# Flamingo gated cross-attention: two of the additions of the softmax sums are made by adding transfers issued from GpSimd

## The chip, the cores and the metric

The kernel runs on one core of a Trainium2 chip. The metric is the device time of one execution in microseconds. The kernel before takes 2557.49 us (median of 2 runs, 2556.8 and 2558.18).

## The reference

Four batches of 256 query rows attend to 1601 context rows each, with 32 query heads of width 128 that share 8 key and value heads, in float32. A gated feed-forward block with eight low-rank experts follows.

```python
x = x + tanh(g_xattn[0]) * xattn(layernorm(x), ctx_4096, Wq, bq, Wkv, bkv, Wo, bo)
x = x + tanh(g_ffn[0]) * ffn(layernorm(x), base_W, router_W, lora_A, lora_B)

# xattn
q = (query @ Wq + bq).reshape(B, L, NKV, G, HDIM)
k_, v_ = split(kv @ Wkv + bkv, 2, axis=-1)          # reshaped to (B, Lk, NKV, HDIM)
scores = einsum('blkgd,bmkd->bkglm', q, k) * scale
attn = softmax(scores, axis=-1)
o = einsum('bkglm,bmkd->blkgd', attn, v).reshape(B, L, NHEAD * HDIM)
return o @ Wo + bo
```

The change touches the denominators of the softmax: for every query row and head, the sum of the exponentials over 1601 keys.

## The kernel before, in words

**Groups.** One group is a key `(b, h, l)`: a batch, a key head and a half of the 256 query rows. There are 4 x 8 x 2 = 64 groups. A group has 4 heads x 128 rows = 512 columns (`W`), and the 1601 keys lie on the partitions in 13 tiles: one of 65 rows and twelve of 128. The twelve go in pairs, so a group has 7 pieces, j = 0 (the 65 rows alone) and j = 1 to 6 (two key tiles each, a tile `p` of 128 x 2 x 512 float32, 512 KB).

**Score phase.** `run_group(cur, prev)` alternates pieces of the current group's scores (`score_unit`, L1142: TensorE writes `sc` to PSUM, ScalarE copies it to `p` in L1151, VectorE folds `p` into a running maximum `mx`, L1067, L1070, L1073) with pieces of the previous group's product with the values (`av_unit`, L1233).

**Softmax.** `softmax(key)` then lets VectorE reduce `mx` across partitions and spread the result (`spread`, L1106 to L1100, five steps), subtract it from every `p` (L1181), and ScalarE take the exponentials (L1184). The sums of the exponentials are pieces in a queue `sum`: `sum_piece(key, j)` calls `fold`, where j = 2 adds `p[1]`, `p[2]` (L1067) and `p[0]` (L1070) into a tile `sm` of 128 x 2 x 512, and j = 3, 4, 5, 6 each add one more `p` (L1073). After the last, `sum_spread` puts the five spreading steps of `sm` in the queues: L1106 adds the halves, L1107 transposes blocks, L1086 reduces and GpSimd copies quadrants (L1090); L1093 and L1209 reduce and invert, GpSimd copies again (L1097); L1100 spreads the result to `rb`. `normalize` (L1292) multiplies the product with it. There is one buffer of `sm`, one of `mx`, and 9 of `p`. The last two keys, `(3, 7, 0)` and `(3, 7, 1)`, have no spreading of `sm`: TensorE sums it across partitions with a matrix of ones (L1257, `su_steps`), and the last key's j = 6 is never folded.

**Projections.** Between score phases `window` runs steps of tasks on TensorE: the query, key and value projections (L896, L907) and the output projection (L484, L1310). A projection pair works with seven products and three PSUM banks; ScalarE copies some products out (L941, L944) and VectorE adds others to them (L951), and TensorE writes on into a bank after such an evacuation has read it.

**Order.** The order of instructions on TensorE, VectorE and ScalarE is fixed while the program is built. A planner keeps a clock for each of them. `later` queues a piece with an engine, a duration in ns, and a key that it waits for; `take` runs the piece, moves the engine's clock by the duration, and marks the piece's own key as done at the end plus `SEM` (200 ns). `fit`, `pump` and `force` take pieces from the heads of the queues, the earliest possible start first, and of equal starts the earlier queue in the list `sub, oT, so, exp, ln, T, norm, sum, low, low_a`. The engines then execute in that order, each instruction behind its semaphores, whatever the real times are. GpSimd's queue holds the small copies of the spreading (six a group), a few memsets (L533, L663) and a few loads (L231 to L234, L558, L601); the large loads and stores are issued from SyncE.

Of the kernel before, what the change touches and what calls it, by code (L numbers as in the profile page):

```python
# [12 lines left out]
ALU = mybir.AluOpType  # L13
# [14 lines left out]
def flamingo_kernel(  # L28
# [51 lines left out]
    nc = tc.nc  # L80
# [16 lines left out]
    NPAIR = len(pairs)  # L97
# [20 lines left out]
    SEM = 200  # L118
    GP_COPIES = 800
    FIT = 300  # L120
    NEVER = math.inf
    clock = {"now": 0.0, "v": 0.0, "a": 0.0, "hold": 0.0}
    free = [0.0] * NBANK
    done = {}
    queues = {q: deque() for q in ("sub", "oT", "so", "exp", "ln", "T", "norm", "sum", "low", "low_a")}

    def vec(ns, ready=None):

        clock["v"] = max(clock["v"], clock["now"] + SEM if ready is None else ready) + ns
        return clock["v"] + SEM  # L130
# [5 lines left out]
    def later(queue, engine, ns, ready, fn, key=None):  # L136

        queues[queue].append((engine, ns, ready, fn, key))

    def start_of(piece):  # L140
        engine, _, ready, _, _ = piece
        if not isinstance(ready, float):
            ready = done.get(ready, NEVER)
        return max(clock[engine], ready)

    def take(q):

        piece = q.popleft()
        engine, ns, _, fn, key = piece
        start = start_of(piece)  # L150
        fn()
        clock[engine] = start + ns
        if key is not None:
            done[key] = start + ns + SEM + (GP_COPIES if key[0] == "part" and key[2] < 4 else 0)

    def pump(until=NEVER, most=None):

        n = 0
        while most is None or n < most:
            heads = [(start_of(q[0]), i, q) for i, q in enumerate(queues.values()) if q]  # L160
            if not heads:
                return n
            start, _, q = min(heads)
            if start == NEVER or start + min(q[0][1], 1200) / 2 > until:
                return n
            take(q)
            n += 1
        return n
# [78 lines left out]
    def mm_cost(n):  # L247

        return 2 * (max(n, P) / 1.2 + 2)
# [809 lines left out]
    p_t, oT_t, rb_t, av_t, po_t = {}, {}, {}, {}, {}  # L1059

    def fold(acc, op, j, key):


        p = p_t[key]
        first = NPAIR - FULL // 2
        if j == first + 1:
            nc.vector.tensor_tensor(acc, p[first], p[first + 1], op)  # L1067
            if first:
                r = rows[-1]
                nc.vector.tensor_tensor(acc[:r, 0, :], acc[:r, 0, :], p[0][:r, 0, :], op)  # L1070
                return 1930
        elif j > first + 1:
            nc.vector.tensor_tensor(acc, acc, p[j], op)  # L1073
        else:
            return 0
        return 1220

    def spread(acc, op, nm, res, after=None, eng=nc.vector):

        q = small.tile([P, 4, NB], F32, tag="quad", name=f"quad_{nm}", bufs=2)
        m = small.tile([P, NB], F32, tag="quadm", name=f"quadm_{nm}", bufs=2)

        def quadrants():
            nc.vector.tensor_reduce(  # L1086
                q[:, 0, :], acc[:, 1, :].rearrange("p (c k) -> p c k", k=32), AX.X, op
            )
            for a in range(1, 4):
                eng.tensor_copy(q[:32, a, :], q[32 * a : 32 * a + 32, 0, :])  # L1090

        def whole():
            nc.vector.tensor_reduce(m[:32], q[:32].rearrange("p a c -> p c a"), AX.X, op)  # L1093
            if after is not None:
                after(m[:32])
            for a in range(1, 4):
                eng.tensor_copy(m[32 * a : 32 * a + 32], m[:32])  # L1097

        def back():
            nc.vector.transpose(  # L1100
                res.rearrange("p (c k) -> p c k", k=32), m.unsqueeze(2).to_broadcast([P, NB, 32])
            )

        own = 550 if eng is nc.vector else 0
        return [
            (690, lambda: nc.vector.tensor_tensor(acc[:, 0, :], acc[:, 0, :], acc[:, 1, :], op)),  # L1106
            (710, lambda: nc.vector.transpose(acc[:, 1, :], acc[:, 0, :])),  # L1107
            (690 + own, quadrants),
            (250 + own + (270 if after is not None else 0), whole),
            (710, back),  # L1110
        ]
# [47 lines left out]
    acc_t, sum_t, late, ring = {}, {}, [], []  # L1159
# [4 lines left out]
    def softmax(key):  # L1164

        nm = "_".join(map(str, key))
        while queues["sub"]:
            pump(most=1)
        mb = pool.tile([P, W], F32, tag="mb", name=f"mb_{nm}", bufs=1)
        for ns, fn in spread(acc_t[key], ALU.max, f"mx_{nm}", mb):  # L1170
            fn()
            vec(ns, clock["v"])

        clock["hold"] = clock["v"] + 1500 - 3 * mm_cost(W)
        for j, tiles in enumerate(pairs):
            n, r = len(tiles), rows[tiles[-1]]
            p = p_t[key][j][:r, :n, :]

            def sub(p=p, r=r, n=n):
                m = mb[:r].unsqueeze(1).to_broadcast([r, n, W])  # L1180
                nc.vector.tensor_tensor(p, p, m, ALU.subtract)  # L1181

            def exp(p=p):
                nc.scalar.activation(p, p, AF.Exp, scale=scale)  # L1184

            later("sub", "v", 1140 if n > 1 else 690, clock["v"], sub, ("sub", key, j))
            later("exp", "a", 1060 if n > 1 else 630, ("sub", key, j), exp, ("exp", key, j))
            if key == last and j == NPAIR - 1:
                continue
            first = NPAIR - FULL // 2  # L1190
            ns = 0 if j <= first else 1230 if j > first + 1 else 1970 if first else 1230
            later("sum", "v", ns, ("exp", key, j), lambda j=j: sum_piece(key, j), ("sum", key, j))
        if key not in tail_keys:
            later("sum", "v", 0, 0.0, lambda: sum_spread(key), ("sums", key))

    def sum_piece(key, j):
        if j == 0:
            nm = "_".join(map(str, key))
            tag = "mx" if key == last else "sm"
            acc_t[key] = pool.tile([P, 2, W], F32, tag=tag, name=f"sm_{nm}", bufs=1)  # L1200
        fold(acc_t[key], ALU.add, j, key)

    def sum_spread(key):

        nm = "_".join(map(str, key))

        rb_t[key] = pool.tile([P, W], F32, tag="rb", name=f"rb_{nm}", bufs=1)
        parts = spread(
            acc_t[key], ALU.add, f"sm_{nm}", rb_t[key], lambda m: nc.vector.reciprocal(m, m), nc.gpsimd  # L1209
        )  # L1210
        for i, (ns, fn) in reversed(list(enumerate(parts[:3]))):
            queues["sum"].appendleft(("v", ns, 0.0, fn, ("part", key, i)))
        for i in (3, 4):
            later("norm", "v", parts[i][0], ("part", key, i - 1), parts[i][1], ("part", key, i))
        later("norm", "v", 690, ("av", key), lambda: normalize(key), ("norm", key))
# [72 lines left out]
    def normalize(key):  # L1288
        b, h, l = key
        oT = pool.tile([P, NQ, P], F32, tag="oT", name=f"oT_{'_'.join(map(str, key))}")  # L1290
        flat = oT.rearrange("p q k -> p (q k)")
        nc.vector.tensor_tensor(flat, av_t[key], rb_t[key], ALU.mult)  # L1292
        later(
            "oT", "a", 720, clock["v"] + 690 + SEM + 500,
            lambda: nc.scalar.activation(flat, flat, AF.Identity, bias=bias_of("v", h)),
            ("oT", key),
        )
        oT_t[key] = oT
        give(clock["v"] + 690 + SEM)
# [302 lines left out]
    class Task:  # L1602
# [14 lines left out]
        def ready(self):  # L1617
            _, ready, _, takes = (self.steps[0] + (False,))[:4]
            if isinstance(ready, (tuple, str)):
                t = done.get(ready, NEVER)  # L1620
            elif isinstance(ready, list):
                t = max(done.get(r, NEVER) for r in ready)
            else:
                t = self.end + ready
            return max(t, min(free, default=NEVER)) if takes else t

# [347 lines left out]
```

## Time and profile before

| what | value |
|---|---|
| runs | 2556.8 and 2558.18 us, median 2557.49 |
| profiled execution, first to last instruction | 2555.5 us, 2.0 us under the median of the runs |
| TensorE busy | 2547.3 us |
| VectorE busy | 2202.6 us |
| ScalarE busy | 1188.1 us |
| GpSimd busy | 150.4 us |
| granted TensorE clock | 1.000 |
| moved by SyncE's queue | 164.41 MB, 19.3% of the 16 DMA engines' span |
| moved by GpSimd's queue | 0.81 MB, 0.1% |
| additions into `sm` of 128 x 1024 (L1073) | 252 in groups 1 to 63, 1220 ns each |

The profile is of one execution. Its span runs from the first to the last instruction of the program, and the rest of a run's time lies around it. A row of a group of instructions gives the line, the engine, the operation, what is written and read, the count, the busy time in us, the mean of one in ns, and the idle time of the engine just before them with what ended most of it. In a timeline the first two numbers are the start and the duration in us. A row of a wait gives the engine and line that waited, what released it, and the total, the number and the longest of such waits. In a list of DMA issues the last number is the median time from the issue to the landing. "PE" is TensorE, "DVE" VectorE, "ACT" ScalarE, "POOL" GpSimd, "SP" SyncE.

### The profile page before, as it was taken

How to read it: one execution, taken by the hardware profiler on the slowest of the kernel's cores; microseconds unless marked ns; L12 is line 12 of the kernel's file. 1: busy time of each engine (PE TensorE's matmuls, PEld its weight loads, DVE VectorE, ACT ScalarE, POOL GpSimd, SP SyncE). 2: the span in 40 equal slices, each digit the busy share in tenths (PEclk: the TensorE clock that was granted, in tenths of full speed). 3: DMA queues.
4: the chain of work that ended last, by engine and by line, in shares of the span. 5: the costliest groups of instructions: out<-in, count | busy, mean ns of one | idle time of the engine just before them, and what ended most of it. 6: DMA issues, size and time to landing. Idle time of an engine off the chain costs nothing.

```text
span 2555.5 us, 26175 instructions
## 1 busy us (share of the span) xinstructions
PE 2547.3 (100%) x9235; PEld 1487.8 (58%) x9235; DVE 2202.6 (86%) x3310; ACT 1188.1 (46%) x1897; POOL 150.4 (6%) x401
## 2 busy tenths in 40 slices
PE   9999999999999999999999999999999999999999
PEld 7557566565555656455565665756656455555554
DVE  4889898899889989899788887878889899998897
ACT  3544454445434555455444444445454445544551
POOL 0000000000000000110000000000000000000000
PEclk9999999999999999999999999999999999999999
DMA  4313222324110111012121111212221011111000
GB/s 158 123 64 108 87 95 84 114 85 149 48 56 23 44 52 56 25 40 83 49 81 37 62 52 62 81 48 81 85 84 56 25 52 52 52 44 52 17 17 33
DMA packets 75499, 167.16 MB, mean 65 GB/s; under 512 B 5372, under 2 KB 32028, under 8 KB 72808
## 3 DMA queue, kind: packets, MB, share of 16 engines
q1 hardware_dynamic: 74424, 164.41, 19.3%
q8 instruction: 73, 1.20, 0.2%
q0 software_dynamic: 416, 0.81, 0.1%
q14 instruction: 58, 0.48, 0.1%
q10 hardware_dynamic: 528, 0.26, 0.0%
HBM read 119.06 MB, written 46.40 MB: 65 GB/s over the span
## 4 chain that ended last, share of the span: by engine, by line
PE 99%; DVE 1%; DMA 0%; ACT 0%; issue 0%; DVEq 0%; ACTq 0%
PE av L1233 28%; PE sc L1142 28%; PE pxk L896 6%; PE pxv L907 6%; PE pxq L896 4%; PE pyk L896 3%; PE pyv L907 3%; PE po L1310 3%; PE pox L484 3%; PE pyq L896 2%; PE pzk L896 2%; PE pzv L907 2%; PE poy L484 1%; PE pzq L896 1%; PE ptv L1020 1%; PE pk L803 1%
## 5 line engine op out<-in xcount | busy, mean ns | idle before, releaser
L1142 PE MATMUL sc<-qT,kT 128*128 128x512 f32 (+1 forms) x1664 | 775.9, 592 | 0.0
L1151 ACT COPY p<-sc 65x512 f32<-65x512 f32 x820 | 474.3, 586 | 636.5 <-PE sc L1142 575.2
L1233 PE MATMUL av<-p,v 65*128 65x512 f32 x1640 | 766.1, 592 | 1.2 <-ACT p L1184 1.2
L1233 PEld LDWEIGHTS av<-p,v 65*128 65x128 f32 x1640 | 309.5, 190 | 376.2 <-issue 370.8
L1142 PEld LDWEIGHTS sc<-qT,kT 128*128 128x128 f32 (+1 forms) x1664 | 307.0, 186 | 374.3 <-issue 340.4
L1181 DVE TENSOR_TENSOR p<-p,mb 65x512 f32<-65x512 f32 x442 | 485.9, 1137 | 0.1
L1184 ACT ACTIVATE p<-p 65x512 f32<-65x512 f32 x442 | 423.1, 990 | 38.6 <-DVE p L1181 34.5
L1073 DVE TENSOR_TENSOR mx<-mx,p 128x1024 f32<-128x1024 f32 x252 | 308.1, 1223 | 137.9 <-ACT p L1151 134.8
L1073 DVE TENSOR_TENSOR sm<-sm,p 128x1024 f32<-128x1024 f32 x252 | 307.4, 1220 | 9.8
L1090 POOL COPY quad_sm<-quad_sm 32x16 f32<-32x16 f32 x186 | 70.7, 380 | 2088.3 <-DVE quad_sm L1086 2083.1
L896 PE MATMUL pxq<-xq,wq 128*128 128x256 f32 x512 | 131.2, 379 | 0.0
L941 ACT ACTIVATE kT<-pxk,biasT 128x384 f32<-128x384 f32 (+1 forms) x120 | 57.9, 508 | 141.8 <-PE pxk L896 141.0
L896 PEld LDWEIGHTS pxq<-xq,wq 128*128 128x128 f32 x512 | 92.5, 189 | 31.2 <-issue 15.3
L941 ACT ACTIVATE qT<-pxq,biasT 128x256 f32<-128x256 f32 x64 | 30.3, 473 | 140.2 <-PE pxq L896 140.2
L944 ACT COPY v<-pxv 128x384 f32<-128x384 f32 x90 | 43.0, 477 | 104.8 <-PE pxv L907 104.8
L896 PE MATMUL pxk<-T,wk 128*128 128x417 f32 (+1 forms) x240 | 90.4, 499 | 0.0
L907 PE MATMUL pxv<-wv,T 128*128 128x128 f32 x720 | 90.2, 275 | 0.0
L896 PE MATMUL pxk<-ctxT,wk 128*128 128x417 f32 (+1 forms) x240 | 90.0, 499 | 0.0
L907 PE MATMUL pxv<-wv,ctxT 128*128 128x128 f32 x720 | 90.0, 275 | 0.0
L907 PEld LDWEIGHTS pxv<-wv,T 128*128 128x128 f32 x720 | 86.4, 192 | 4.7 <-issue 4.3
L907 PEld LDWEIGHTS pxv<-wv,ctxT 128*128 128x128 f32 x720 | 86.4, 192 | 4.7 <-issue 4.3
L1067 DVE TENSOR_TENSOR mx<-p,p 128x1024 f32<-128x1024 f32 x63 | 76.8, 1220 | 13.1 <-ACT p L1151 12.8
(264 smaller groups left out, 2809.6 us busy)
## 6 DMA issues: line engine op xcount, KB each, us to landing
wo<-in_L_xattn_Wo_dram SPq DMA_DIRECT2D x18, 1024.0 KB, 5.3
kept_q<-wq SPq DMA_DIRECT2D x16, 896.0 KB, 4.8
wq<-kept_q SPq DMA_DIRECT2D x16, 896.0 KB, 5.1
wo<-kept_wo SPq DMA_DIRECT2D x13, 1024.0 KB, 5.8
wk<-kept_k SPq DMA_DIRECT2D x11, 896.0 KB, 4.6
wv<-kept_v SPq DMA_DIRECT2D x11, 896.0 KB, 4.4
ctx<-in_ctx_dram SPq DMA_DIRECT2D x36, 256.0 KB, 2.7
wq<-in_L_xattn_Wq_dram SPq DMA_DIRECT2D x32, 256.0 KB, 3.1
```

Source lines behind the costliest of these rows:

```text
L484: nc.tensor.matmul(bk[:, :HD], left[i]()[:, c, :], blk[:, c, :], start=first and c == 0, stop=c == 1, skip_group_check=True,)
L896: nc.tensor.matmul(bk[:, :n], a(SLOT[i], c), operand(i, c, s, n), start=first and c == 0, stop=c == 1, skip_group_check=True,)
L907: nc.tensor.matmul(bk[:, t * HDIM : (t + 1) * HDIM], operand(i, c, s + t * P, P), a(SLOT[i], c), start=first and t == 0 and c == 0, stop=c ...
L941: nc.scalar.activation(dst, src, AF.Identity, bias=bias_of(kind, h0 + f))
L1067: nc.vector.tensor_tensor(acc, p[first], p[first + 1], op)
L1073: nc.vector.tensor_tensor(acc, acc, p[j], op)
L1142: nc.tensor.matmul(sc[:r, :], kT_t[b, h][:, key_col(i) : key_col(i) + r], qT_t[b, h][:, :, l * P : (l + 1) * P], start=True, stop=True,)
L1151: nc.scalar.copy(p[:r, k, :], sc[:r, :])
L1181: nc.vector.tensor_tensor(p, p, m, ALU.subtract)
L1184: nc.scalar.activation(p, p, AF.Exp, scale=scale)
L1233: nc.tensor.matmul(av, v_t[b, h][:r, i, :], p_t[key][j][:r, k, :], start=(j == 0 and k == 0), stop=(j == NPAIR - 1 and k == len(pairs[j]) ...
L1310: nc.tensor.matmul(po, oT_t[key][:, g, :], w_t["o", b, h][:, g, :], start=(g == 0), stop=(g == G - 1),)
```

## The change

For j = 5 and 6, `sum_piece` issues a transfer from GpSimd that adds `p[j]` to `sm` in SBUF, in place of VectorE's addition. In the planner these two pieces take no time of VectorE, and their keys are marked as done `ASIDE_NS` = 5000 ns later than a piece of no duration would be. The first three spreading steps of `sm` now wait for the key of the group's last sum, where before they waited for nothing (they stood at the head of the queue behind that sum). The additions of j = 2, 3 and 4 and all the maxima stay as they are.

```diff
+    ASIDE = (5, 6)
+    ASIDE_NS = 5000
...
         if key is not None:
-            done[key] = start + ns + SEM + (GP_COPIES if key[0] == "part" and key[2] < 4 else 0)
+            late_by = GP_COPIES if key[0] == "part" and key[2] < 4 else 0
+            if key[0] == "sum" and key[2] in ASIDE:
+                late_by = ASIDE_NS
+            done[key] = start + ns + SEM + late_by
...
             first = NPAIR - FULL // 2
-            ns = 0 if j <= first else 1230 if j > first + 1 else 1970 if first else 1230
+            ns = 0 if j <= first or j in ASIDE else 1230 if j > first + 1 else 1970 if first else 1230
             later("sum", "v", ns, ("exp", key, j), lambda j=j: sum_piece(key, j), ("sum", key, j))
...
+        if j in ASIDE:
+            nc.gpsimd.dma_start(acc_t[key], p_t[key][j], accum_op=ALU.add)
+            return
         fold(acc_t[key], ALU.add, j, key)
...
         for i, (ns, fn) in reversed(list(enumerate(parts[:3]))):
-            queues["sum"].appendleft(("v", ns, 0.0, fn, ("part", key, i)))
+            queues["sum"].appendleft(("v", ns, ("sum", key, NPAIR - 1), fn, ("part", key, i)))
```

## The prediction

> **What bounds the kernel now.** I read the busy line of the page first, then the chain that ended last, then the groups of instructions, and last the waits of TensorE.
>
> ```profile
> PE 2547.3 (100%) x9235; PEld 1487.8 (58%) x9235; DVE 2202.6 (86%) x3310; ACT 1188.1 (46%) x1897; POOL 150.4 (6%) x401
> ...
> PE 99%; DVE 1%; DMA 0%; ACT 0%; issue 0%; DVEq 0%; ACTq 0%
> ...
> L1073 DVE TENSOR_TENSOR sm<-sm,p 128x1024 f32<-128x1024 f32 x252 | 307.4, 1220 | 9.8
> ```
>
> TensorE is busy for 2547.3 of 2555.5 us, and 99% of the chain is its own. Its longest wait on another engine is this one:
>
> ```profile
> PE av L1233 <- ACT p L1184: 1.2, 1, 1.2
> ```
>
> All six such waits together are 4.1 us (1.2+1.1+0.8+0.5+0.3+0.2). No matmul is removed, so the most that the change can gain is the 8.2 us in which TensorE isn't busy; I count 3 us of them. VectorE's additions are cover work. The question is whether VectorE, which runs in an order fixed at build time, comes late somewhere.
>
> **What is removed.** 63 groups lose two additions (j = 5 and 6) and the last group loses one: 127 x 1.22 us (the L1073 row) = 155 us of VectorE, 2.44 us a group. It goes from 86% to about 80% busy. On the path this is worth nothing, since TensorE waits for VectorE hardly anywhere.
>
> **What is added.** 127 transfers, each 512 KB read from p, 512 KB read from sm and 512 KB written back. Both transfers of a group change the same sm, so the second can't start before the first has landed, and the first spreading step (L1106 on sm) can't start before the second has. The trace has no adding transfer. Nearest rows of the list of transfers:
>
> ```profile
> wo<-in_L_xattn_Wo_dram SPq DMA_DIRECT2D x18, 1024.0 KB, 5.3
> ...
> xa<-kept_wo SPq DMA_DIRECT2D x9, 512.0 KB, 3.7
> ...
> bo<-in_L_xattn_bo_dram POOLq DMA_DIRECT2D x2, 256.0 KB, 7.4
> ```
>
> Call T the time from issue to landing. Lower end: 3.7 us, a plain 512 KB. Upper end: 9.2 us, the slower of the two POOL-issued 256 KB loads (5.5 and 9.2). I take **5.3 us**, the 1024 KB row, because an adding transfer has to read 1024 KB. The pair of a group then lands 10.6 us after it is issued.
>
> The Trainium skill ("DMA: Bandwidth & Descriptors", "Two DMAs through the same engine are not ordered") says that only the completion semaphore orders two transfers, whatever queue they share, and its rules for kernel authors ask for that wait when transfers add to the same bytes; no row here shows such a pair. The same page ("Anatomy of one DMA") gives about 2.0 us plus bytes/436e3 for a GpSimd-issued transfer, an estimate of 4.4 us for 1 MB; the trace's 1024 KB row from SP is 5.3 us, already above it. By the page the pair would take 8.8 us, and the sum below would come to about 2575 us.
>
> **When the pair starts, and when VectorE wants it.** In the timeline of VectorE I find the end of the fourth addition (j = 4) and the start of the next group's max spread (L1106 on mx). The first group:
>
> ```profile
> 103.40 2.48 DVE L1073 TENSOR_TENSOR sm<-sm,p 128x1024 f32<-128x1024 f32 x2
> 105.79 1.22 DVE L1073 TENSOR_TENSOR mx<-mx,p 128x1024 f32<-128x1024 f32 x1
> 106.93 1.22 DVE L1073 TENSOR_TENSOR sm<-sm,p 128x1024 f32<-128x1024 f32 x1
> 108.18 0.69 DVE L1106 TENSOR_TENSOR sm<-sm 128x512 f32<-128x512 f32 x1
> 109.12 1.23 DVE L1073 TENSOR_TENSOR mx<-mx,p 128x1024 f32<-128x1024 f32 x1 [0.25 <-ACT p L1151]
> 110.26 0.70 DVE L1107 STREAM_TRANSPOSE sm<-sm 128x512 f32<-128x512 f32 x1
> 111.00 0.69 DVE L1086 TENSOR_REDUCE quad_sm<-sm 128x16 f32<-128x512 f32 x1
> 111.61 0.68 DVE L1106 TENSOR_TENSOR mx<-mx 128x512 f32<-128x512 f32 x1
> ```
>
> The fourth addition ends at 104.6 (half of the 2.48 us row). In all 62 groups that have these spreads the exponential of j = 5 is done before that point, and in 56 that of j = 6 as well, so both transfers are ready to go there. The planner takes both pieces at once, at no VectorE time, and marks the sum of j = 6 as done 5.2 us later (200 + 5000 ns): it allows for one transfer, not for two in a row. So it may put the first spreading step 5.2 us after 104.6, at 109.8, and still ahead of the max spread at 111.61. The pair lands at 115.2. VectorE then stands for up to 10.6 - 5.2 = 5.4 us on that step, with the last max fold, the max spread, the subtractions and the evacuations of PSUM queued behind it.
>
> How late the max spread becomes depends on the gap from the end of the fourth addition to it, here 7.0 us. Spreading steps 0 to 2 (0.69 + 0.70 + 0.69 = 2.1 us) still stand ahead of it, so the lateness is the smaller of 5.4 and 12.7 - gap (10.6 + 2.1 = 12.7). Read from the same two rows, the gaps of the 62 groups are: 6 below 5.2 us (2.5 to 3.8; the spread is planned behind the max spread, no stall); 8 of 6.5 to 7.1; 16 of 9.2 to 10.4, mean 9.7; 6 of about 12.1; 26 of 14.8 to 26.1 (the stall lies among folds that wait for scores anyway, no loss). Lateness: 8 x 5.4 + 16 x 3.0 + 6 x 0.6 = 95 us.
>
> **What TensorE sees of it.** Behind the max spread comes the projection stage:
>
> ```profile
> 111.60:130.20 18.60, 17.51 (x36) 1.00 0.17 55
> ```
>
> and, from the timelines of VectorE and TensorE in it:
>
> ```profile
> 116.31 0.42 DVE L951 TENSOR_TENSOR qs_q<-pxq,qs_q 128x256 f32<-128x256 f32 x1
> ...
> 125.05 0.59 DVE L951 TENSOR_TENSOR kT<-pxk,kT 128x417 f32<-128x417 f32 x1
> ```
>
> ```profile
> 118.32 1.02 PE L896 MATMUL pxq<-xq,wq 128*128 128x256 f32 x4
> ...
> 126.18 1.56 PE L896 MATMUL pxk<-ctxT,wk 128*128 128x417 f32 x4
> ```
>
> By the window (start and end, length, VectorE's busy time, clock, DMA share, GB/s) VectorE is busy 17.51 of 18.60 us, so it can make up 1.1 us. The timelines show the margin: TensorE writes pxq again 1.6 us after VectorE has read it (116.73 to 118.32), and pxk 0.5 us after (125.64 to 126.18); all 30 pxk evacuations have 0.46 to 0.54 us. So I let 1.6 us of each lateness vanish (1.1 made up, 0.5 margin), and TensorE stands for the rest: 8 x 3.8 + 16 x 1.4 = 53 us.
>
> **Other parts.** *End of the kernel*: the key (3,7,0) and the last one feed sm to TensorE (L1257, at 2510.38 and 2521.14). For the first, j = 5 and 6 end at 2510.2 now and the pair would land at 2507.6 + 10.6 = 2518.2, 8.0 us later; for the last, one transfer ends at about 2519.5 + 5.3 = 2524.8 and not 2520.7, 4.1 us later. Output products and base products (3.5 and 5.3 us of TensorE) can come first; I charge 5 us, between 0 and 12. *POOL's queue*: the transfers queue with 6 small copies a group, which come behind them and need their result anyway, and with a few instructions that wait long (L663 39.3 us in two waits, L533 19.8, L601 14.0, L558 10.1: 83 us at most, if VectorE stood for all of it); I charge 3, since they are nine among 128 transfers. *SP's queue* is not passed, but its loads share the 16 engines: the DMA share is 0.42 in 92.0 to 111.6, 19% overall. That lengthens T somewhat and stays in its bounds. *Slots of p*: p[5] and p[6] come free when their transfer lands; they are next written in the scores of the group after the next, over 10 us after the landing. Nothing.
>
> **Sum.** 53 + 5 + 3 - 3 = 58 us on the profiled span of 2555.5; the median of the runs is 2.0 us above that span, so 2557.5 + 58 = **2615 us**, 2.3% slower.
>
> **Rivals.**
>
> 1. *The stall is covered* (0.31; not slower). If T is 3.7 us, the plain 512 KB row, the pair lands after 7.4 us: stalls are 2.2 us, less 1.6 us each, so only the 8 short gaps cost anything: 8 x 0.6 = 5 us, and the end of the kernel about 1. Against the gain of 3 us that is 2560; with the stalls absorbed wholly, 2554. It decides as long as 2T stays under 6.8 (5.2 + 1.6) or little above. For it: the 512 KB rows (3.7, 3.6, 2.7 us), and 2.44 us less VectorE work a group. Against: an adding transfer reads twice as much, and GpSimd's issues land later than SP's. At T = 4.7 the same working gives 8 x 2.6 + 16 x 0.2 = 24, in all 2588.
>
> 2. *The transfers are much slower* (0.22). At T = 7.5 the pair takes 15 us: stalls of 9.8 us, lateness the smaller of 9.8 and 17.1 - gap: 8 x 9.8 + 16 x 7.4 + 6 x 5.0 + 12 gaps between 14.8 and 17.1 at about 1.2 = 241, less 1.6 x 42 = 67, so +174 and 2735 with the other parts. For it: the POOL-issued 256 KB loads of 5.5 and 9.2 us. Against: those are early or broadcast loads; POOL's 64 KB loads late in the kernel land after 2.9. The forecast passes into this case at T = 6.4 (8 x 6.0 + 16 x 3.6 + 6 x 1.2 = 113, 2677).
>
> 3. *POOL's queue is the bound* (0.02): transfers stand behind POOL's long waits and VectorE behind them, 83 us: 2640 with T at 3.7.
>
> **Chances.** The forecast case, T from 4.7 to 6.4 (2588 to 2677), has 0.45. 2% is 51 us, about what a measurement of this kernel can tell from no change; it is passed at T of about 5.2, so 0.31 of the 0.45 lie above. Slower: 0.31 + 0.22 + 0.02 = 0.55; faster by 2% would need 51 us where TensorE is idle for 8: 0.01; within 2%: 0.44. The range leaves out the slow end of rival 2 and the very fast end of rival 1: 2556 to 2740.
>
> **What would show it.** In the profile after: L1073 on sm with 127 fewer instructions, VectorE's busy time about 155 us lower; 127 POOL-issued rows of 512 KB landing after about 5.3 us; waits of the second transfer on the first; a new wait of VectorE at L1106 on sm for a transfer, some 100 us or more in total; and waits of TensorE for VectorE in the projection stages, some 50 us. If L1106 waits but TensorE's idle time stays near 8 us, my 1.6 us of cover is too small. If T is off, everything scales with it. If the planner puts the spreading steps behind the max spread where I put them ahead, the stalls are gone whatever T is.

## The result and the profile after

The changed kernel takes 2775.46 us (median of 2 runs, 2768.68 and 2782.24) where the kernel before takes 2557.49: 1.085 times as long, 95% interval 1.0785 to 1.0914. The forecast was 2615 us in a range of 2556 to 2740. The sign was right, and the loss was 218 us where 58 had been forecast.

The profiled execution took 2768.68 us and spans 2766.9 us, 211.4 us more than the span before. The busy line, the chain and the groups that matter, from the page of the changed kernel:

```profile
PE 2617.6 (95%) x9235; PEld 1524.4 (55%) x9235; DVE 2045.4 (74%) x3183; ACT 1190.7 (43%) x1895; POOL 276.0 (10%) x528
...
PE 5%; DVE 2%; DMA 1%; issue 0%; ACT 0%; POOL 0%; DVEq 0%; POOLq 0%; ACTq 0%
...
L1207 POOL DMA_DIRECT2D sm<-p x126 | 108.3, 860 | 1676.5 <-ACT p L1156 1070.3
L1111 DVE TENSOR_TENSOR sm<-sm 128x512 f32<-128x512 f32 x62 | 42.9, 691 | 306.8 <-DMA sm<-p 306.8
...
L1078 DVE TENSOR_TENSOR sm<-sm,p 128x1024 f32<-128x1024 f32 x126 | 153.4, 1217 | 5.5 <-ACT p L1189 0.5
...
sm<-p POOLq DMA_DIRECT2D x126, 512.0 KB, 4.5
```

VectorE has 127 fewer instructions (3310 to 3183) and 157 us less work. TensorE has the same 9235 matmuls, but is idle for 149.3 us where it was idle for 8.2, and is busy for 70.3 us longer with the same work. The chain of the changed kernel was followed back over less than a tenth of the span, so I don't argue from its shares. The new cost stands in the L1111 row: VectorE waits 306.8 us for transfers to land before the first spreading step of `sm`. (The lines have moved by 5 to 8: L1111 is the former L1106, L1156 the former L1151, L1078 the former L1073, L956 the former L951, L901 the former L896.)

The waits of TensorE, which came to 4.1 us before:

```profile
PE pxq L901 <- DVE qs_q L956: 52.9, 23, 5.1
PE pxv L912 <- DVE v L956: 24.7, 7, 4.7
PE poy L489 <- DVE xa L495: 17.5, 7, 5.0
PE pxk L901 <- DVE kT L956: 14.3, 6, 4.0
PE pyk L901 <- ACT kT L946: 12.9, 4, 4.4
PE su L1265 <- DMA sm<-p: 5.4, 1, 5.4
```

Most are waits for VectorE's evacuations in the projection stages. One group, the fifth, on GpSimd and then on VectorE:

```profile
279.02 0.86 POOL L1207 DMA_DIRECT2D sm<-p  x1 [33.73 <-issue]
284.10 0.86 POOL L1207 DMA_DIRECT2D sm<-p  x1 [4.22 <-ACT p L1156]
```

```profile
277.28 1.21 DVE L1078 TENSOR_TENSOR sm<-sm,p 128x1024 f32<-128x1024 f32 x1
278.42 1.21 DVE L1078 TENSOR_TENSOR mx<-mx,p 128x1024 f32<-128x1024 f32 x1
281.06 1.23 DVE L1078 TENSOR_TENSOR mx<-mx,p 128x1024 f32<-128x1024 f32 x1 [1.43 <-ACT p L1156]
288.67 0.69 DVE L1111 TENSOR_TENSOR sm<-sm 128x512 f32<-128x512 f32 x1 [6.38 <-DMA sm<-p]
...
293.07 1.15 DVE L1078 TENSOR_TENSOR mx<-mx,p 128x1024 f32<-128x1024 f32 x1
294.77 0.71 DVE L1105 STREAM_TRANSPOSE rb<-quadm_sm 128x512 f32<-128x512 f32 x1 [0.55 <-POOL quadm_sm L1102]
295.40 0.65 DVE L1111 TENSOR_TENSOR mx<-mx 128x512 f32<-128x512 f32 x1
```

The fourth addition ends at 278.5, the first transfer starts at 279.02, the second 5.1 us later, when the first has landed, and the second lands at 288.6. VectorE has come to the first spreading step at 282.3 and stands there for 6.38 us. Behind it are two folds and the rest of the spreading, so the max spread starts at 295.40. TensorE then runs into it:

```profile
295.72 1.56 PE L901 MATMUL pxk<-ctxT,wk 128*128 128x417 f32 x4
300.95 2.07 PE L901 MATMUL pxq<-xq,wq 128*128 128x256 f32 x4 [3.67 <-DVE qs_q L956]
302.81 2.26 PE L901 MATMUL pzk<-ctxT,wk 128*128 128x417 f32 x4
```

It waits 3.67 us, and the next four matmuls take 2.07 us where four of the same form took 1.02 at 118.32 in the kernel before. The window behind the gap has the reason in its third column from the right (start and end, length, busy time of TensorE, its weight loads, VectorE, ScalarE and GpSimd, granted clock, DMA share, GB/s):

```profile
300.80:304.20 3.40, 3.25 (x6) 2.18 (x7) 3.40 (x5) 2.26 (x5) 0.00 (x0) 0.50 0.01 4
```

The granted clock is half for 3.4 us. The trace has 28 such stretches between TensorE's first and last matmul, and TensorE is busy in them for 108.3 us; at half clock, half of that, 54.1 us, is lost. Before there was none. So the 211.4 us are 141.1 us of TensorE standing (149.3 - 8.2), 54.1 us of half clock, and 16.2 us more of TensorE's busy time. These go with the number of gaps: the busy time of TensorE is in 74 pieces where it was in 9, so each gap more comes with 0.25 us of busy time (0.23 to 0.28 in the runs below with one transfer, four additions, the plan of 7.5 us and the work at the first step). Why a gap adds that isn't shown.

One more measure is used below. I call **lateness** the time from the end of a group's last score copy (L1156) to the start of its max spread, over the mean of that in the kernel before, 1.7 us. Over the 64 groups it sums to 197 us in the changed kernel.

### The profile page after: what moved, and what is told of

It reads as the page before. It is cut to its first block, busy times and chain, and to the rows that moved or that the text cites. A ratio compares the mean times of both kernels' runs of the same rounds, so it can differ in the third digit from the quotient of the medians.

```text
span 2766.9 us, 26467 instructions
## 1 busy us (share of the span) xinstructions
PE 2617.6 (95%) x9235; PEld 1524.4 (55%) x9235; DVE 2045.4 (74%) x3183; ACT 1190.7 (43%) x1895; POOL 276.0 (10%) x528
## 5 line engine op out<-in xcount | busy, mean ns | idle before, releaser
L1156 ACT COPY p<-sc 65x512 f32<-65x512 f32 x820 | 474.5, 586 | 651.4 <-PE sc L1147 599.5
L1078 DVE TENSOR_TENSOR mx<-mx,p 128x1024 f32<-128x1024 f32 x252 | 305.7, 1213 | 121.1 <-ACT p L1156 116.5
L1207 POOL DMA_DIRECT2D sm<-p x126 | 108.3, 860 | 1676.5 <-ACT p L1156 1070.3
L1111 DVE TENSOR_TENSOR sm<-sm 128x512 f32<-128x512 f32 x62 | 42.9, 691 | 306.8 <-DMA sm<-p 306.8
L901 PE MATMUL pxq<-xq,wq 128*128 128x256 f32 x512 | 138.9, 395 | 53.0 <-DVE qs_q L956 52.9
L1078 DVE TENSOR_TENSOR sm<-sm,p 128x1024 f32<-128x1024 f32 x126 | 153.4, 1217 | 5.5 <-ACT p L1189 0.5
L901 PEld LDWEIGHTS pxq<-xq,wq 128*128 128x128 f32 x512 | 94.0, 194 | 92.3 <-DVE qs_q L956 64.1
L1095 POOL COPY quad_sm<-quad_sm 32x16 f32<-32x16 f32 x186 | 81.5, 438 | 569.0 <-DVE quad_sm L1091 563.9
L912 PE MATMUL pxv<-wv,ctxT 128*128 128x128 f32 x720 | 100.2, 294 | 24.7 <-DVE v L956 24.7
L912 PEld LDWEIGHTS pxv<-wv,ctxT 128*128 128x128 f32 x720 | 95.6, 209 | 31.5 <-DVE v L956 26.1
L901 PE MATMUL pxk<-ctxT,wk 128*128 128x417 f32 (+1 forms) x240 | 97.9, 534 | 14.5 <-DVE kT L956 14.3
L901 PE MATMUL pxk<-T,wk 128*128 128x417 f32 (+1 forms) x240 | 91.1, 502 | 0.0
```

The costliest lines, as they stand in the source:

```text
L901: nc.tensor.matmul(bk[:, :n], a(SLOT[i], c), operand(i, c, s, n), start=first and c == 0, stop=c == 1, skip_group_check=True,)
L912: nc.tensor.matmul(bk[:, t * HDIM : (t + 1) * HDIM], operand(i, c, s + t * P, P), a(SLOT[i], c), start=first and t == 0 and c == 0, stop=c ...
L1156: nc.scalar.copy(p[:r, k, :], sc[:r, :])
L1207: nc.gpsimd.dma_start(acc_t[key], p_t[key][j], accum_op=ALU.add)
```

## The experiments

The theory after the result: the planner allows 5.2 us for a pair that takes 10.2, VectorE stands for the rest, and its lateness reaches TensorE as idle time and then as half clock. The rivals were that the traffic and GpSimd's issues slow the rest, and that the new order itself is bad. All times are medians of executions beside the kernel before (2557.1 to 2557.6 us in the three sets).

"Lost to half clock" is half of TensorE's busy time in the stretches of half clock.

| run | us | ratio, 95% interval | wait at L1111, us | lateness, us | TensorE idle, us | lost to half clock, us |
|---|---|---|---|---|---|---|
| changed kernel | 2775.5 | 1.0849 (1.0785 to 1.0914) | 306.8 | 197 | 149.3 | 54.1 |
| pair planned at 10.3 us | 2570.7 | 1.0052 (1.0037 to 1.0067) | 29.1 | 2 | 17.2 | 0 |
| additions left out | 2561.3 | 1.0015 (1.0005 to 1.0024) | 0 | -4 | 12.0 | 0 |
| transfers to another tile | 2564.1 | 1.0026 (1.0016 to 1.0036) | 0 | -2 | 14.8 | 0 |
| one transfer | 2576.6 | 1.0076 (1.0061 to 1.0091) | 68.7 | 25 | 21.8 | 0 |
| two additions not planned | 2563.7 | 1.0024 (1.0015 to 1.0034) | 0 | 6 | 12.9 | 0 |
| four additions not planned | 2629.5 | 1.0282 (1.0266 to 1.0297) | 0 | 95 | 59.7 | 8.8 |
| pair planned at 7.5 us | 2618.2 | 1.0237 (1.0220 to 1.0254) | 135.6 | 90 | 52.7 | 6.8 |
| plain transfers | 2611.0 | one run | 142.9 | 64 | 45.8 | 6.8 |
| work at the first step | 2825.6 | 1.1048 (1.1033 to 1.1064) | 0 | 217 | 185.2 | 74.2 |

**Planning the pair.**

```diff
-    ASIDE_NS = 5000
+    ASIDE_NS = 10300
```

> The same transfers; the planner is told 10.3 us in place of 5.0, the time in which a pair landed in the changed kernel (about 10.2 us from the end of the fourth addition). Theory (VectorE stands at the first spreading step because one transfer's time was planned for two in a row, and all the rest follows from that): VectorE's wait at L1111 for a transfer falls from 306.8 us to under 40, TensorE's idle time from 149 us to under 30, its clock is granted in full nearly everywhere, 2555 to 2585 us. Rival (the 66 MB more on the DMA engines and GpSimd's queue slow the rest): the transfers are all there, so over 2700 us.

2570.7 us. One constant takes back 205 of the 218 us, with all 127 transfers in place. From this run's waits:

```profile
DVE mx L1078 <- ACT p L1156: 231.5, 159, 2.7
POOL sm L1207 <- DMA sm<-p: 203.1, 45, 6.2
...
DVE sm L1111 <- DMA sm<-p: 29.1, 16, 8.0
```

The second transfer still waits for the first as long as before (4.5 us on average in both: 203.1 us in 45 waits of GpSimd here, 160.8 us in 36 in the changed kernel), but VectorE hardly waits for them any more and is back to waiting for scores. The rival of traffic falls here. This run also gets another order of instructions, so it doesn't show by itself that the order was harmless.

**The order alone.** The pieces of j = 5 and 6 do nothing. The sums lack four key tiles.

```diff
         if j in ASIDE:
-            nc.gpsimd.dma_start(acc_t[key], p_t[key][j], accum_op=ALU.add)
             return
```

> Leaves out the additions of j = 5 and 6 altogether (the sums lack four key tiles); the planner and so the order on TensorE, VectorE and ScalarE are those of the changed kernel. Theory: without a landing to wait for, the order by itself is harmless, 2550 to 2565 us. Rival (the order that the planner makes with two pieces of no VectorE time, the spreading ahead of the max spread, is what costs): 2700 us or more.

2561.3 us. With the order of the changed kernel, but nothing to wait for, 3.7 us are lost. The order is not the cause.

**The transfers without the wait.** They add to a tile in DRAM that nobody reads (the first one writes it).

```diff
-            nc.gpsimd.dma_start(acc_t[key], p_t[key][j], accum_op=ALU.add)
+            flat = p_t[key][j].rearrange("p t w -> p (t w)")
+            nc.gpsimd.dma_start(aside[0], flat, **({"accum_op": ALU.add} if aside[1:] else {}))
+            aside.append(key)
             return
```

> The transfers add p to a tile in DRAM in place of sm, so VectorE waits for none of them (the sums lack four key tiles); the order is that of the changed kernel, GpSimd issues as many transfers of 512 KB, one after the other as before. Theory: 2550 to 2575 us. Rival (traffic and GpSimd's issues): over 2700 us. With part of the loss from traffic: in between, and the part can be read off.

2564.1 us: 2.8 us over the run before, so 127 transfers of 512 KB, their issues and their landing (5.4 us here) cost about that much by themselves. They go to HBM in this run and to SBUF in the changed kernel; that difference was not tried. Their row in the list of DMA issues:

```profile
aside<-p POOLq DMA_DIRECT2D x126, 512.0 KB, 5.4
```

**One transfer for the time that was planned for one.** Only j = 6 is a transfer, and VectorE adds j = 5 in time that the plan doesn't know.

```diff
-        if j in ASIDE:
+        if j == 6:
             nc.gpsimd.dma_start(acc_t[key], p_t[key][j], accum_op=ALU.add)
```

> Order and plan of the changed kernel, but j = 5 is added by VectorE (1.22 us that the plan does not know) and only j = 6 by a transfer, which is what the 5.0 us allow for. Theory: the wait at L1111 falls from 5.4 us a group to 1 to 2 us, TensorE's gaps get too short to lower its clock, 2560 to 2620 us. Rival (traffic): half of the transfers, half of the loss, about 2665 us. Rival (order): as the changed kernel, about 2770 us.

2576.6 us, in the range of the theory and far from half of the loss. The wait is 1.6 us on average in 43 groups, and no clock is lost.

**How much lateness is covered.** Here VectorE makes the additions itself, in the changed kernel's order.

```diff
-        if j in ASIDE:
-            nc.gpsimd.dma_start(acc_t[key], p_t[key][j], accum_op=ALU.add)
-            return
         fold(acc_t[key], ALU.add, j, key)
```

> No transfers: VectorE makes the additions of j = 5 and 6 itself, but the plan and so the order are those of the changed kernel, in which these take no time of VectorE. VectorE is late by 2.44 us a group, with no wait for any landing. By the prediction's working (1.6 us of each lateness vanish) some 57 x 0.8 = 46 us, about 2605 us; if the score phase covers more than that, 2560 to 2580 us; if it covers nothing, 2557 + 57 x 2.4 = about 2695 us and half clock on top.

2563.7 us: the 2.44 us a group that the plan doesn't know are covered almost wholly. My working would have given 2605. Each addition made twice (the sums count four key tiles twice):

```diff
         if j in ASIDE:
-            nc.gpsimd.dma_start(acc_t[key], p_t[key][j], accum_op=ALU.add)
-            return
+            fold(acc_t[key], ALU.add, j, key)
         fold(acc_t[key], ALU.add, j, key)
```

> As the run with two additions, but each is made twice (the sums count four key tiles twice): 4.88 us a group that the plan does not know, near the 5.4 us that VectorE stands in the changed kernel. Theory (any lateness of VectorE of that size at that place does it, whether it waits or works): 2700 to 2790 us, of which 40 to 70 us by a lower TensorE clock after gaps. Rival (the wait for a transfer does more than hold VectorE): under 2650 us.

2629.5 us. This was a miss for the theory as I had put it, and in the range of its rival: 4.88 us of work cost 72 us, and 5.4 us of standing cost 218. The timeline of VectorE in the same group as above shows what differs:

```profile
263.14 6.25 DVE L1078 TENSOR_TENSOR sm<-sm,p 128x1024 f32<-128x1024 f32 x5
269.32 2.55 DVE L1078 TENSOR_TENSOR mx<-mx,p 128x1024 f32<-128x1024 f32 x2
271.78 0.69 DVE L1111 TENSOR_TENSOR sm<-sm 128x512 f32<-128x512 f32 x1
```

The four extra additions (of the five in the first row) run right behind the fourth addition, in the 5.2 us that the plan leaves for the transfer, where VectorE has two folds and idle time. The stall of the changed kernel begins after that time is spent. To settle it, the work was put where the stall is.

**The same time, at the place of the stall.** No transfers and no additions of j = 5 and 6; 5.6 us of VectorE's work directly ahead of the first spreading step.

```diff
+        halves = parts[0][1]
+        def stand():
+            a = acc_t[key]
+            for _ in range(4):
+                nc.vector.tensor_tensor(a, a, a, ALU.max)
+            nc.vector.tensor_tensor(a[:, 0, :], a[:, 0, :], a[:, 0, :], ALU.max)
+            halves()
+        parts[0] = (parts[0][0], stand)
```

> No transfers and no additions of j = 5 and 6 (the sums lack four key tiles), order of the changed kernel; directly ahead of the first spreading step VectorE works for 4 x 1.22 + 0.69 = 5.6 us on sm (maxima of a tile with itself), where in the changed kernel it stands for 5.4 us on average. Theory (VectorE's lateness at this place is the whole cause; six microseconds of work earlier, in the time that the plan leaves for the transfer, cost less because VectorE has idle time there): 2720 to 2800 us, TensorE idle 110 to 160 us, 40 to 75 us lost to a lower clock. Rival (a transfer in flight does something beyond holding VectorE): as the run with four additions, 2600 to 2660 us.

```profile
286.58 5.00 DVE L1223 TENSOR_TENSOR sm<-sm 128x1024 f32<-128x1024 f32 x4
291.61 0.69 DVE L1224 TENSOR_TENSOR sm<-sm 128x512 f32<-128x512 f32 x1
292.34 0.69 DVE L1111 TENSOR_TENSOR sm<-sm 128x512 f32<-128x512 f32 x1
```

2825.6 us, over the range that I had given (2720 to 2800). The work stands in all 62 groups, the stall in 57, and it is 0.2 us longer. TensorE's waits have the form of the changed kernel's:

```profile
PE pxq L901 <- DVE qs_q L956: 53.7, 19, 5.3
PE pxk L901 <- DVE kT L956: 39.7, 11, 5.7
PE pxv L912 <- DVE v L956: 24.2, 7, 5.1
```

So no transfer is needed for the loss. VectorE held for that long at that place is enough, whatever holds it. What counts is the place, not VectorE's total: this kernel's VectorE is busy for 85% of the span, and with four additions it was 89% and lost a quarter as much. The work here is 0.7 us a group longer than the four additions; over 62 groups that is 43 us, and the lateness differs by 122 us.

**Half of the stall.** The transfers of the changed kernel, planned at 7.5 us.

```diff
-    ASIDE_NS = 5000
+    ASIDE_NS = 7500
```

> The transfers of the changed kernel, planned at 7.5 us in place of 5.0: the pair lands about 2.5 us after the plan's time. Theory: wait at L1111 about 57 x 2.5 = 140 us or less, TensorE's gaps mostly under 2 us, so its clock is granted in full but for a few stretches, 2575 to 2640 us; less than half of the loss for half of the stall, since the cover takes the first part and the clock gate the last.

2618.2 us. The wait is 44% of the changed kernel's (135.6 of 306.8 us), and the loss 28% (60.8 of 218 us). TensorE's idle time grows by 44.5 us (141.1 there), and half clock takes 6.8 us (54.1 there).

**What the adding costs.** Plain copies over `sm`, which makes the sums wrong.

```diff
-            nc.gpsimd.dma_start(acc_t[key], p_t[key][j], accum_op=ALU.add)
+            nc.gpsimd.dma_start(acc_t[key], p_t[key][j])
```

> The transfers copy p over sm and add nothing (the sums are wrong); everything else as in the changed kernel. Tells what the adding costs. If a transfer's time goes by the bytes read, a plain one of 512 KB lands about 1 us sooner than the adding one (4.5 us), about 3.5 us; if it is set by GpSimd's issue and fixed parts, it lands in 4.3 us or more. Time 2650 to 2775 us, the less the sooner they land.

The two rows of transfers, first of the plain run, then of the changed kernel:

```profile
L1207 POOL DMA_DIRECT2D sm<-p x126 | 66.9, 531 | 1620.4 <-ACT p L1156 1049.3
```

```profile
L1207 POOL DMA_DIRECT2D sm<-p x126 | 108.3, 860 | 1676.5 <-ACT p L1156 1070.3
```

The issue takes 0.53 us in place of 0.86, and the landing is 2.9 us in place of 4.5 after the start of the issue (medians). The adding costs 1.6 us a transfer. A plain one landed sooner than both ways of expecting had it (3.5, or 4.3 and more), and the time, 2611.0 us in a single execution, is below the range that I had given (2650 to 2775).

**What is left, and two attempts to use the freed time.** Pair planned at 10.3 us, and the last two keys summed by VectorE:

```diff
-        if j in ASIDE:
+        if j in ASIDE and key not in tail_keys:
```

(and the same condition for the planner's duration and landing time)

> As the run with the pair planned at 10.3 us, but the two last keys, whose sums TensorE reads at the end of the kernel, are summed by VectorE alone as before. Theory (half or more of the 13 us that are left there lie in the last 100 us, where the landing is on the path): 2556 to 2565 us. Rival (they come from 124 transfers beside the other loads): 2567 to 2572 us.

2566.5 us, ratio 1.0034 (1.0021 to 1.0048): 4 us better than with the last keys, and a miss, since I had looked for half or more of the 13 us. About 9 us stay over the kernel before. Order and traffic by themselves made 3.7 and 2.8 us above, in another order; what makes up the rest stays open.

On top of it, more heads of the output projection in seven products in place of eight: `N_BLOCK` 8, 3, 8, 4 and 7, 4, 8, 5 in place of 6, 3, 7, 4.

> As the run without the last keys, and three more heads of batches 0 and 2 take the output projection with seven block products in place of eight (N_BLOCK 8, 3, 8, 4 in place of 6, 3, 7, 4): by the rows about 0.86 us less of TensorE a head and some more of VectorE. If the VectorE time that the transfers free can be turned into something: 2 to 3 us below that run, 2554 to 2562 us; if VectorE or its loads come late, over it.

> As the run before, with N_BLOCK 7, 4, 8, 5: four more heads by blocks, about 3.4 us less of TensorE. 2553 to 2561 us if the work fits; over 2563 us if not.

2571.8 us (1.0044 to 1.0069) and 2570.1 us (1.0036 to 1.0061). Neither gains, and both miss what I had expected, though VectorE has some 130 us less to do than in the kernel before (2068.5 and 2072.0 us). Both have one wait of TensorE that the run without them doesn't have (this is the line of the first; the second has the same):

```profile
PE pxk L901 <- ACT kT L946: 6.0, 1, 6.0
```

With the half clock behind it (1.7 and 1.5 us), it makes 7.7 and 7.5 us. By my estimate they would take about 2564 and 2563 us without it, 2 to 4 us less than the run that they build on; that was not tried. No version here beats the kernel before.

## Why the prediction was wrong, point by point

- **What bounds the kernel: right.** TensorE is the bound, and 157 us less on VectorE bought nothing in any run.
- **The transfers: right for the pair, partly by luck.** T was taken as 5.3 us and the pair as 10.6 us from the end of the fourth addition. Measured: landing 4.5 us after the issue, the issues 5.1 us apart, the pair 10.2 us (105.1 to 115.3 in the first group). T was 0.8 us too long, and the 0.5 to 0.6 us that pass ahead of each issue were left out; the two errors nearly cancel. The wait of the second for the first, on which the Trainium skill ("DMA: Bandwidth & Descriptors", "Two DMAs through the same engine are not ordered") insists, is there with 160.8 us in 36 waits on GpSimd.
- **The planner allows for one transfer of the two: right.** Up to 5.4 us of stall were forecast, the mean is 5.4 us in 57 groups (0.7 to 13.5), and planning the pair removes nine tenths of it (29.1 us are left).
- **Which groups come late: wrong.** This is the step "the smaller of 5.4 and 12.7 - gap", with "26 of 14.8 to 26.1 (the stall lies among folds that wait for scores anyway, no loss)". In its order of gaps before (6.5 to 7.1, 9.2 to 10.4, about 12.1, 14.8 and more, under 5.2) I had forecast a lateness of 43, 48, 4, 0 and 0 us, in all 95. Measured, each group against itself in the kernel before, are 30, 67, 26, 69 and 5 us, in all 198. The term that was too small is the 2.1 us of work behind the landing: in the fifth group, 6.7 us pass from the landing to the max spread (288.7 to 295.4), since the folds that came due in the stall and the last spreading steps, with their waits for GpSimd's copies, stand there too. Over the groups in which the step waits, it is 2.8, 4.7, 5.9 and 9.5 us on average in the first four kinds. And the long gaps were no shelter, since VectorE is busy for most of the time behind the step there too. In the run without the additions, in those 26 groups, VectorE is idle for 4.7 of the 12.6 us from the step to the max spread. In the changed kernel the step comes 6.0 us later, and 3.0 of the 4.7 us are used up; the rest is lateness. The runs with work in place of the stall agree: 4.88 us ahead of the stall's place made 95 us of lateness, 5.6 us at its place 217.
- **What TensorE sees of a lateness: about right.** I had let it stand for 53 of 95 us, 0.56; measured are 135 us idle in these groups for 198 us of lateness, 0.68.
- **The clock: left out.** The sum had no term for it. 54.1 us of half clock are nearly as much as the whole forecast loss of 58. I had taken TensorE's lost time as the sum of its waits; the 16.2 us of busy time that come with the gaps were left out too.
- **The end of the kernel: about right.** It was charged 5 us. TensorE waits there for a transfer once, 5.4 us (L1265), and giving the last two keys back to VectorE saved 4 us (with the pair planned at 10.3 us).
- **The rivals.** The number of the second (2735 us at T = 7.5) is nearest to the result, but its mechanism is wrong: the landing was 4.5 us. Contention in GpSimd's queue is not seen either: in 60 of 62 groups the first transfer is issued within 0.6 us of the fourth addition's end. The first, that the stall is covered, is what happens when the plan is told 10.3 us. The sums for other values of T are up to 4 us off by their own terms (2578, 2586, 2676 and 2736 us, where about 2575, 2588, 2677 and 2735 were given); nothing hangs on that.

## What to carry to other kernels

Where engines run in an order fixed at build time, moving work to a transfer is as good as the landing time that the plan assumes, and two transfers into the same tile land one after the other, so the plan needs the time of both. A stall on an engine that isn't the bound is priced at its place: ask what is queued behind it there and who needs that soon, and not how idle the engine is on average. When the engine that is the bound does stand, add the clock that it loses afterwards (here 54 us beside 141 us of standing).

## What the runs showed of the hardware

A gap on TensorE costs more than its length. In the changed kernel all 19 gaps of 3.3 us and more were followed by half clock or ran into it, 9 of the 17 between 2.0 and 2.9 us as well, and none of the 9 between 1.0 and 1.7 us. The stretches last 3.4 us or twice that. Two gaps over 3 us inside other runs had none (3.6 us in the run planned at 7.5 us, 3.2 us in the run with work at the first step), so the length of a gap alone doesn't settle it.

What does settle it is where the gap lies. In each trace the stretches begin on a fixed grid of 3.413 us: the first three of the changed kernel begin at 205.2, 300.8 and 389.5 us, the second and third 28 and 54 steps behind the first, and the others fit as well. I cut all traces into the windows of their grids and add up TensorE's idle time in each. Of the windows at full clock, 78 were followed by half clock: 77 of them had 1.94 to 3.41 us idle, one 1.70. None of the others had more than 1.98. The 3.6 us gap was split by the grid into 1.76 and 1.80 us, and the 3.2 us gap into 1.27 and 1.90. Within half clock less was enough: the 26 windows that were followed by another at half clock had 0.70 us idle or more, the 78 after which the clock came back 0.58 or less.

The Trainium skill ("TensorE: Matmul & The Clock Gate", "Part 1: The HAM clock gate") describes a gate that looks at free-running windows of about 3.4 us, and its rules ("Why this matters for your kernels") ask for no gaps over about 3 us. The length of the stretches and the grid agree; the gaps of 2.0 to 2.9 us show that keeping to that rule is not enough here. In the run with 5.6 us of work at the first step half clock took 74.2 us, 28% of the loss of 268.

An adding transfer of 512 KB from SBUF to SBUF lands 4.5 us after its issue from GpSimd, a plain one after 2.9 us, and 0.33 us of the difference lie in the issue itself (0.86 and 0.53 us). One into a tile in DRAM lands after 5.4 us. The issue of an adding transfer is also visible as busy time of GpSimd: 109 us of the rise from 150.4 to 276.0.
